# A schedule written out by hand: one pair of the gated block a round later, and the expert groups 4, 2, 2 in place of 2, 4, 2

## The chip, the cores and the metric

The kernel runs on one core of a Trainium2 chip. The metric is the device time of one execution in microseconds, taken as the median of several executions. Engines are named as the profile names them: PE is TensorE (PEld its weight loads), DVE is VectorE, ACT is ScalarE, POOL is GpSimd and SP is SyncE, which here only issues DMAs.

## The reference

The input is 8 sequences of 512 tokens with 128 features. Eight layers follow each other, each added to its input after a layer norm: a recurrence with a circulant matrix, a perceptron with a low-rank addition, a four-layer encoder with linear attention, the same perceptron, and then the four that matter here:

```python
x = x + _L1_attn_a_ref(_layernorm(x), ...)   # causal attention and a perceptron
x = x + _L1_ffn_ref(_layernorm(x), ...)      # experts, first block
x = x + _L1_attn_b_ref(_layernorm(x), ...)   # gated linear attention
x = x + _L1_ffn_ref(_layernorm(x), ...)      # experts, second block
```

In an expert block each token chooses 2 of 8 experts by a router's scores; an expert is `val * silu(gate)` with 352 hidden units and a product back to 128 features, and the two results are added with their softmax weights. The gated block has a short convolution, a gated linear attention in chunks with 64 keys and 256 values, and a normalised product back to 128 features:

```python
h = jnp.einsum('bsd,ehd->bseh', xn, w_up)
val, gate = jnp.split(h, 2, axis=-1)
h = val * jax.nn.silu(gate)
y = jnp.einsum('bseh,edh->bsed', h, w_down)
```

## The kernel before, in words

All eight sequences stay on the chip as one tile `x`; a sequence is four tiles of 128 tokens. The layers up to the first expert block run one after the other and are not touched. What is told here is the last part: the end of the first expert block, the gated block and the second expert block, which are interleaved by hand in `gated_and_experts`.

**An expert block** (`Experts`) splits the sequences into groups (`GROUPS`: the first block 4 and 4, the second 2, 4 and 2 sequences). For each group, in this order:
- `steps(b)` normalises a sequence and makes its router scores (lines 982 to 1035).
- `choose(g)` finds the two experts of each token of the group and the row of each in a list that is sorted by expert. It is a chain of small DVE instructions with two PE products in it (lines 1038 to 1148), in 12 steps.
- `posts(many)` is a stream of indirect DMAs from POOL, one a step. A *slots post* (L1159) writes the rows of one tile of 128 tokens to the sorted list in DRAM, twice for each tile of the group: 16 posts for two sequences, 32 for four. A *given post* (L1171) writes one finished tile's rows back to the order of the tokens. `behind` makes each post wait for the PE instruction that was written last before it.
- `tiles(g)` computes the sorted rows, 128 at a time, with the weights of one expert: 23 tiles for two sequences, 39 for four. It is cut into *pieces*: the first only fetches (`xr`, an SP DMA from the sorted list that waits until every slots post of the group has landed), then one piece for each tile, then two that only finish what is under way. A tile is two products with the up weights (L1274 and L1275), an activation, two DVE products (L1287, L1288), three transposes (L1238), a copy, and the product with the down weights (L1247). Every fourth tile begins with the transposes of a fetched `xr` (L1218).
- `combine(g)` loads the results of each sequence (`y`) and adds them to `x` on DVE (L1324, eight for a sequence); for the second block it also writes the output.

**The gated block** works on pairs of sequences. `gated_steps` gives each pair 25 steps, and the second expert block's `steps` add four. They are named here by their age in the pipeline:
- *norm* (age -1, 2 steps): statistics and normalisation of the two sequences.
- *main* (age 0, 15 steps): transposes (L1630), the up product and a convolution of three DVE instructions each (L1640, L1641, L1647), silu, `vt` (L1678, L1685), the key, query and gate products (L1665), `tau` to `u` on ACT (L1692 to L1696), a series of ten DVE instructions in `u` (L1702, L1704) that ends in `g` (L1720), squares, `pn` (L1725) and `g_nn` (L1731), the logarithm and a scan (L1730 to L1753), `vt` once more with a product (L1760, L1763), and `ke`, `qe` (L1767, L1768).
- *second* (age 1, 8 steps): scores and states (L1776 to L1797), the gate `sg` (L1806, L1807), outputs (L1816 to L1823), the product back and its norm (L1828, L1833, L1837, with a power on POOL through L164 and L165), and the addition to `x` (L1845).
- *end* (age 2, 4 steps): the second expert block's `steps` for the two sequences (L993 to L1031, with a power on POOL, L999).

`pipeline` runs rounds; in each it goes through the list `ages`, 29 places, and at a place with age a it advances the pair that started a rounds ago. Pair 0 has its main step in round 0, pair 1 in round 1, and so on; norms come a round earlier. After each place it also advances a side stream, which `dealt` makes from `tiles`, `posts`, `combine` and `choose`: each has a set of places at which it is advanced, written as `at(round, places)`. `fast(stream, n)` takes n steps at once, `whole` runs a stream to its end. What is left of the side stream after the last round is run alone.

Inside this block `in_program_order` keeps PE, DVE, ACT and POOL each in the order in which the program is written, so that the order above is the order on each engine. Only posts of one kind and group are free among themselves. SP's DMAs are issued in order too.

Afterwards `blend` runs the remaining pieces of the second block's tiles together with given posts and the `combine` of the first two groups; the last group's `combine` is alone at the end.

Of the kernel before, what the change touches and what calls it, by code (L numbers as in the profile page):

```python
# [20 lines left out]
B = 8  # L21
# [1 line left out]
D = 128  # L23
NT = S // P

GROUPS = ((4, 4), (2, 4, 2))
MOST = max(max(g) for g in GROUPS)


# [24 lines left out]
def pipeline(make, count, ages, side=None, every=0, first=0):  # L54

    live = {}
    done = 0
    for now in range(min(ages), count + max(ages)):  # L60
        for age in ages:
            n = now - age
            if 0 <= n < count:
                if n not in live:
                    live[n] = make(n)
                next(live[n], None)
            done += 1
            if side is not None and now >= first and done % every == 0:
                next(side, None)
# [5 lines left out]
@contextmanager  # L75
def in_program_order(tc, *loose):


    block = tc.nc.cur_bb
    first = len(block.bb.instructions)  # L80
    yield
    assert tc.nc.cur_bb is block
    engines = (mybir.EngineType.PE, mybir.EngineType.DVE, mybir.EngineType.Activation, mybir.EngineType.Pool)
    last = {}
    for i in block.bb.instructions[first:]:
        if i.engine in engines:
            group = next((one[i.name] for one in loose if i.name in one), None)
            before = last.setdefault(i.engine, {})
            for other, names in before.items():
                if group is None or other != group:  # L90
                    for name in names:
                        tc.add_manual_dep(i, name, ORDER, reason="the order in which it is written")
            if group is None:
                before.clear()
            before.setdefault(group, []).append(i.name)
# [302 lines left out]
def encoder_block(k):  # L398
# [5 lines left out]
    with tc.tile_pool(name="enc1", bufs=1) as one, tc.tile_pool(name="enc", bufs=2) as pool:  # L404
# [150 lines left out]
        with in_program_order(tc):  # L555
            pipeline(
                steps,
                L * B,
                (2, 0, -1, 3, -2, 1, 0, 2, -1, 4, 1, 0, 2, 1, 0, 2, 1, 0, 3, -2),
            )  # L560
# [340 lines left out]
def blend(*streams):  # L901


    live = [[iter(one), 0, n] for one, n in streams]
    while live:
        one = min(live, key=lambda l: (l[1] + 1) / l[2])
        one[1] += 1
        if next(one[0], live) is live:
            live.remove(one)


def blank_slots(k, groups):

    nc, tc = k.nc, k.tc
    slots = []
    for i, seqs in enumerate(groups):
        n = tiles_of(seqs)
        one = tc.dram_tile([n * P, D + 2], F32, name=f"slots{i}")  # L920
        nc.sync.dma_start(one.rearrange("(t p) d -> p t d", p=P), k.blank[:, None, :].to_broadcast([P, n, D + 2]))
        slots.append((seqs, one, tc.dram_tile([2 * MOST * S + n * P, D], F32, name=f"given{i}")))
    return slots
# [407 lines left out]
def chain(*streams):  # L1331
    for one in streams:
        yield from one


def run(stream):
    for _ in stream:
        pass


def fast(stream, *many):

    while True:
        for n in many:
            for _ in range(n):
                if next(stream, stream) is stream:
                    return
            yield


def idle(many):
    yield from range(many)


def take(stream, many):

    for _ in range(many):
        if next(stream, stream) is stream:
            return
        yield  # L1360


def until(true):

    while not true():
        yield


def whole(stream):

    for _ in stream:
        pass
    yield


def dealt(*streams):

    streams = [(iter(stream), set(steps)) for stream, steps in streams]
    for q in range(1 + max(max(steps) for _, steps in streams)):
        for stream, steps in streams:  # L1380
            if q in steps:
                next(stream, None)
        yield
# [7 lines left out]
def in_turn(m):  # L1391


    streams = [(m.tiles(g), turns(g) - (g.number > 0)) for g in m.groups]

    def pieces():
        for i, (stream, n) in enumerate(streams):
            for at in range(n):
                if at == n - 3 and i + 1 < len(streams):
                    next(streams[i + 1][0])  # L1400
                next(stream)
                yield

    return pieces(), sum(n for _, n in streams)
# [75 lines left out]
def gated_and_experts(k, before, posts, slots, keep, banks, out):  # L1480

    tc = k.tc
    first, last = before.groups
    with tc.tile_pool(name="moe1", bufs=1, side="right") as room:
        m = Experts(k, "n", slots, keep, room, before.p3, out)
        m.hids = before.hids
        one, two, three = m.groups
        tiles, pieces = in_turn(m)
        own = m.posts(sum(2 * g.n + g.tiles for g in m.groups))
        with tc.tile_pool(name="gla1", bufs=1) as alone, tc.tile_pool(name="gla", bufs=2) as pool:  # L1490
            with k.banks(**banks["gated"]):
                gated = gated_steps(k, alone, pool)

                def steps(pair):
                    yield from gated(pair)
                    for _ in zip(m.steps(2 * pair), m.steps(2 * pair + 1)):
                        yield

                ages = (0, 0, 1, 0, 1, 1, 0, 2, 1, 1, 0, 2, 0, 2, 0, -1, 1, 0, 2, 0, 0, 1, -1, 0, 1, 0, 0, 0, 0)

                def at(now, *places):
                    return [(now + 1) * len(ages) + i for i in places]

                side = dealt(  # L1510
                    (before.tiles(last), at(-1, 4, *range(7, 29)) + at(0, *range(0, 29, 2)) + at(1, *range(4))),
                    (posts, at(-1, *range(29)) + at(0, *range(29)) + at(1, *range(6))),
                    (posts, at(-1, *range(9))),
                    (whole(posts), at(1, 6)),
                    (before.combine(first), at(-1, *range(9, 18))),
                    (before.combine(last), at(1, *range(8, 15), 17, 19)),
                    (m.choose(one), at(2, *range(19, 29)) + at(3, *range(3))),
                    (own, at(3, *range(3, 29)) + at(4, *range(29)) + at(5, *range(32))),
                    (own, at(5, *range(0, 32, 2))),
                    (tiles, at(3, *range(20, 29, 2)) + at(4, *range(0, 29, 4)) + at(5, *range(0, 32, 4))),  # L1520
                    (fast(m.choose(two), 2), at(4, *range(19, 26))),
                    (m.choose(three), at(5, *range(19, 32))),
                )
                with in_program_order(tc, before.loose, m.loose):
                    pipeline(steps, B // 2, ages, side=side, every=1)
                    run(side)
        with k.banks(**banks["experts"]), in_program_order(tc, m.loose):
            left = pieces - 21

            def combined(g):  # L1530
                yield from until(lambda: len(g.back) == g.tiles)
                yield from idle(3)
                yield from m.combine(g)

            blend((tiles, left), (take(fast(own, 1, 2), left), left), (chain(*(combined(g) for g in m.groups[:2])), left))
            run(own)
            run(m.combine(three))


def moe_block(k, slots, out=None):  # L1540

    tc = k.tc
    with ExitStack() as stack:
        keep, room = (
            stack.enter_context(tc.tile_pool(name=name, bufs=1, side="right")) for name in ("moe", "moe1")
        )
        m = Experts(k, "m", slots, keep, room, stack.enter_context(tc.tile_pool(name="moe3", bufs=1)), out)
        m.hidden()
        with in_program_order(tc, m.loose):
            for g in m.groups:  # L1550
                pipeline(lambda i: m.steps(g.first + i), g.seqs, (0, -1, 0, 1))
                run(m.choose(g))
                run(m.posts(2 * g.n))
                blend((m.tiles(g), turns(g)), (m.posts(g.tiles), turns(g)))
                run(m.combine(g))
# [538 lines left out]
def net_kernel(ctx: ExitStack, tc: tile.TileContext, drams, offsets, out):  # L2094
# [38 lines left out]
    w_a.close()  # L2133
    slots = [blank_slots(k, one) for one in GROUPS]
    with k.banks(**usual):
# [40 lines left out]
    with tc.If(large > 0):  # L2176
        nc.sync.dma_start(flat, saved)
        slots = [blank_slots(k, one) for one in GROUPS]
        again = ExitStack()
# [228 lines left out]
```

## Time and profile before

| | us |
|---|---|
| median of 7 runs | 2028.75 |
| lowest and highest of them | 2020.35, 2031.98 |
| the profiled execution's own time | 2027.83 |
| its span, first to last instruction | 2026.1 |

| engine | busy us | share of the span |
|---|---|---|
| PE | 1739.6 | 86% |
| PEld | 1180.9 | 58% |
| DVE | 1286.4 | 63% |
| ACT | 948.5 | 47% |
| POOL | 730.8 | 36% |

A busy share is the union of an engine's instructions. Matmuls are pipelined and their ends are modelled, so a busy PE is not PE at its peak. The granted clock is the share of TensorE's full clock that its throttle let through; it was 0.908 over the whole span. A row of a stretch gives its bounds, its length, and each engine's busy time in it (with the number of instructions), then the granted clock, the share of the DMA engines and GB/s. A wait names the instruction that stood, what ended the wait, the sum, the number and the longest. In time lines the columns are start, length, engine, line, operation and tiles; a bracket holds how long the engine had stood before the instruction, and what ended that.

### The profile page before, as it was taken

Reading aid. Unit: us, or ns where it says so; the run is one execution under the profiler, and the core shown is the slowest. Engines: PE = TensorE matmul, PEld = TensorE weight load, DVE = VectorE, ACT = ScalarE, POOL = GpSimd, SP = SyncE. Lnnn points to the kernel's source line nnn. Section 1 sums busy time; section 2 is a strip of 40 time slices with the busy share of each in tenths; the row PEclk is TensorE's granted clock in tenths of the full one; section 3 lists DMA queues with packets and bytes.
Section 4 is the critical chain, followed back from the end, with each engine's and each line's share of the span. In section 5 each row is a group of like instructions: output and inputs, shape, how many; then the busy total and the mean of one; then the engine's idle time right before and its main releaser. Section 6 shows DMA issues by size and latency. Waiting matters only on the chain. (4 is left out here: it accounts for less than half of the span.)

```text
span 2026.1 us, 29976 instructions
## 1 busy us (share of the span) xinstructions
PE 1739.6 (86%) x10171; PEld 1180.9 (58%) x10171; DVE 1286.4 (63%) x4211; ACT 948.5 (47%) x1703; POOL 730.8 (36%) x866
## 2 busy tenths in 40 slices
PE   4998789999998779799999887876989886877995
PEld 2655567788786645344444445654656554655774
DVE  7654788888886664576566635635747775464564
ACT  1022466666664422356556463544554562443553
POOL 2111333333334340244444474561313210447632
PEclk9888799999998878899899898988998886878998
DMA  9900000000000020100000002122100100102332
GB/s 250 162 1 1 1 1 1 1 1 1 1 1 0 1 92 1 42 1 1 1 1 1 9 28 70 57 65 66 39 10 12 48 1 2 50 31 85 100 105 65
DMA packets 79390, 71.25 MB, mean 35 GB/s; under 512 B 6560, under 2 KB 73120, under 8 KB 78336
## 3 DMA queue, kind: packets, MB, share of 16 engines
q1 hardware_dynamic: 69120, 47.89, 9.8%
q0 software_dynamic: 9536, 20.47, 3.0%
q8 instruction: 86, 1.41, 0.3%
q10 hardware_dynamic: 576, 0.90, 0.1%
q14 instruction: 72, 0.59, 0.1%
HBM read 34.98 MB, written 34.25 MB: 34 GB/s over the span
## 5 line engine op out<-in xcount | busy, mean ns | idle before, releaser
L165 POOL TENSOR_TENSOR ln_rs<-rs_v,mhalf 128x4 f32<-128x4 f32 x144 | 150.5, 1046 | 430.6 <-DVE rs_v L164 417.2
L1171 POOL DMA_INDIRECT given<-yr,to x163 | 160.1, 982 | 307.1 <-PE ps_a L1274 110.6
L679 ACT ACTIVATE pr<-ps_s 128x1024 f32<-128x1024 f32 x160 | 154.7, 1019 | 120.9 <-PE ps_s L669 120.8
L1287 DVE SCALAR_TENSOR_TENSOR half<-half,ps_a 128x352 f32<-128x352 f32 x163 | 84.6, 519 | 167.2 <-ACT half L1280 167.0
L1159 POOL DMA_INDIRECT slots<-xn,rpos x128 | 124.4, 972 | 69.8 <-issue 26.0
L1275 PE MATMUL ps_a<-w_m,xt 128*128 x326 | 131.9, 488 | 18.4 <-DVE half L1287 9.9
L669 PE MATMUL ps_s<-qm,rot 32*128 32x128 f32 (+3 forms) x1024 | 124.2, 488 | 23.6 <-ACT pr L679 23.5
L1274 PE MATMUL ps_a<-w_m,xt 128*128 x326 | 135.1, 498 | 7.2 <-ACT xt L1220 5.7
L683 POOL TENSOR_SCALAR_AFFINE_SELECT pr<-pr 128x256 f32<-128x256 f32 x256 | 100.1, 416 | 112.5 <-ACT pr L679 108.3
L530 PEld LDWEIGHTS ps_c<-w_e,mlp_g 128*128 128x128 f32 x1024 | 126.6, 198 | 15.1 <-issue 14.8
L530 PE MATMUL ps_c<-w_e,mlp_g 128*128 128x128 f32 x1024 | 128.8, 281 | 0.1
L1240 ACT COPY gt<-ps_b 128x384 f32<-128x384 f32 x163 | 77.9, 478 | 102.4 <-PE ps_b L1238 102.4
L522 PE MATMUL ps_a<-zt,w_e 128*128 128x512 f32 x256 | 123.7, 607 | 0.9 <-ACT zt L211 0.9
L1280 ACT ACTIVATE half<-ps_a 128x352 f32<-128x352 f32 x163 | 75.5, 463 | 82.7 <-PE ps_a L1274 81.9
L178 DVE BATCH_NORM_AGGREGATE ln_mv<-ln_st 128x2 f32<-128x6 f32 x576 | 100.1, 178 | 16.3
L669 PEld LDWEIGHTS ps_s<-qm,rot 32*128 32x128 f32 x1024 | 59.9, 194 | 82.1 <-ACT pr L679 55.6
L373 ACT ACTIVATE mlp_g<-ps_a,w_col 128x512 f32<-128x512 f32 x64 | 44.0, 687 | 125.5 <-PE ps_a L372 124.8
L523 ACT ACTIVATE mlp_g<-ps_a,w_col 128x512 f32<-128x512 f32 x128 | 85.7, 687 | 35.3 <-PE ps_a L522 35.3
L224 POOL TENSOR_TENSOR xe<-xe,w_erow 128x512 f32<-128x512 f32 x64 | 82.3, 1306 | 55.2 <-DVE ks L480 52.8
L1275 PEld LDWEIGHTS ps_a<-w_m,xt 128*128 128x128 f32 x326 | 62.9, 199 | 63.7 <-DVE half L1287 16.9
L1238 PEld LDWEIGHTS ps_b<-w_ident,hid 128*128 128x128 f32 x489 | 63.5, 145 | 61.9 <-issue 26.9
L211 ACT ACTIVATE zt<-ps_b,w_col 128x512 f32<-128x512 f32 x80 | 62.7, 784 | 75.5 <-PE ps_b L204 75.4
(385 smaller groups left out, 4067.4 us busy)
## 6 DMA issues: line engine op xcount, KB each, us to landing
xr<-slots SPq DMA_DIRECT2D x37, 260.0 KB, 3.0
y<-given SPq DMA_DIRECT2D x32, 256.0 KB, 3.7
slots<-blank SPq DMA_DIRECT2D x3, 2535.0 KB, 29.1
w_m<-in_m_dram SPq DMA_DIRECT2D x2, 2244.0 KB, 10.6
w_e<-in_e_dram SPq DMA_DIRECT2D x2, 1700.0 KB, 11.0
slots<-blank SPq DMA_DIRECT2D x2, 1495.0 KB, 30.6
given<-yr,to POOLq DMA_INDIRECT x163, 2.2
x<-in_u_dram SPq DMA_DIRECT2D x8, 256.0 KB, 9.5
```

Of the source, the lines that this page charges most:

```text
L165: nc.gpsimd.tensor_tensor(out, v, self.mhalf[:, :n], ALU.pow)
L178: nc.vector.bn_aggr(mv[:, t, :], st[:, t, :])
L522: nc.tensor.matmul(ph, w1[:, c * P : (c + 1) * P], ht, start=True, stop=True)
L523: nc.scalar.activation(g[:, c, :], ph, AF.Relu, bias=col["e_b1"][:, l, c : c + 1])
L530: nc.tensor.matmul(py[:, t, :], g[:, c, t * P : (t + 1) * P], w2[:, c, :], start=(c == 0), stop=(c == 3))
L669: nc.tensor.matmul(halves[g // 2][:, g % 2, at : at + S - u * P], kr[rows, u * P : (u + 1) * P], qm[rows, i, u * P : S], start=True, stop= ...
L679: nc.scalar.activation(pr, sc, AF.Exp)
L683: nc.gpsimd.affine_select(out=v, in_=v, pattern=[[0, 2], [1, P]], compare_op=ALU.is_ge, fill=0.0, base=0, channel_multiplier=-1,)
L1159: made = nc.gpsimd.indirect_dma_start(out=g.slots, out_offset=bass.IndirectOffsetOnAxis(ap=g.pos[:, i, t : t + 1], axis=0), in_=g.xn[:, t, :],
L1171: made = nc.gpsimd.indirect_dma_start(out=g.given, out_offset=bass.IndirectOffsetOnAxis(ap=to, axis=0), in_=yr, in_offset=None,)
L1274: nc.tensor.matmul(pg, xt, w["experts"][:, bass.ds(o + HID, HID)], start=True, stop=True)
L1275: nc.tensor.matmul(pv, xt, w["experts"][:, bass.ds(o, HID)], start=True, stop=True)
```

## The change

`pipeline` takes a list of the rounds in which the pairs start in place of their number. The gated block's pairs now start in rounds 0, 1, 3 and 4. The first block's second group of tiles, until now dealt over two rounds and four places, is spread over three, and its posts and `combine` come later. The second block's groups are 4, 2 and 2 sequences in place of 2, 4 and 2; `choose` of the first group is taken two steps at a time, its 32 slots posts follow, and the tiles stand at every second place of the last round and of what is run after it, until 31 pieces (21 before) are done. Sizes, instructions and transfers of a tile, a pair or a post stay as they are.

```diff
-GROUPS = ((4, 4), (2, 4, 2))
+GROUPS = ((4, 4), (4, 2, 2))
...
-    for now in range(min(ages), count + max(ages)):
+    starts = {start: n for n, start in enumerate(range(count) if isinstance(count, int) else count)}
+    for now in range(min(ages), 1 + max(starts) + max(ages)):
         for age in ages:
-            n = now - age
-            if 0 <= n < count:
+            n = starts.get(now - age)
+            if n is not None:
...
                 side = dealt(
-                    (before.tiles(last), at(-1, 4, *range(7, 29)) + at(0, *range(0, 29, 2)) + at(1, *range(4))),
-                    (posts, at(-1, *range(29)) + at(0, *range(29)) + at(1, *range(6))),
+                    (before.tiles(last), at(-1, 4, *range(7, 23)) + at(0, *range(0, 29, 2)) + at(1, *range(0, 28, 3))),
+                    (posts, at(-1, *range(29)) + at(0, *range(29)) + at(1, *range(29))),
                     (posts, at(-1, *range(9))),
-                    (whole(posts), at(1, 6)),
+                    (whole(posts), at(2, 1)),
                     (before.combine(first), at(-1, *range(9, 18))),
-                    (before.combine(last), at(1, *range(8, 15), 17, 19)),
-                    (m.choose(one), at(2, *range(19, 29)) + at(3, *range(3))),
-                    (own, at(3, *range(3, 29)) + at(4, *range(29)) + at(5, *range(32))),
-                    (own, at(5, *range(0, 32, 2))),
-                    (tiles, at(3, *range(20, 29, 2)) + at(4, *range(0, 29, 4)) + at(5, *range(0, 32, 4))),
-                    (fast(m.choose(two), 2), at(4, *range(19, 26))),
-                    (m.choose(three), at(5, *range(19, 32))),
+                    (before.combine(last), at(2, *range(3, 12))),
+                    (fast(m.choose(one), 2), at(3, *range(19, 26))),
+                    (own, at(3, *range(26, 29)) + at(4, *range(29)) + at(5, *range(29)) + at(6, *range(32))),
+                    (tiles, at(5, 0, *range(2, 29, 2)) + at(6, *range(0, 32, 2))),
+                    (fast(m.choose(two), 2), at(5, *range(19, 26))),
+                    (fast(m.choose(three), 2), at(6, *range(19, 26))),
                 )
...
-                    pipeline(steps, B // 2, ages, side=side, every=1)
+                    pipeline(steps, (0, 1, 3, 4), ages, side=side, every=1)
...
-            left = pieces - 21
+            left = pieces - 31
```

## The prediction, made before the run

> **What bounds the kernel now.** I read the page's slices first, then a table of stretches that I cut at the last product of each main step (DVE's `qe`, L1768), then the waits and the time lines of PE, POOL and DVE at the joints between stretches.
>
> From the page, PE's busy tenths and the granted clock in 40 slices:
>
> ```profile
> PE   4998789999998779799999887876989886877995
> ...
> PEclk9888799999998878899899898988998886878998
> ```
>
> PE is the engine to follow; in the last third (slices 27 to 38, everything that the change touches) it falls to 6 and 7 in two places. The table of stretches says where:
>
> ```profile
> core 0: us, PE busy (x) PEld busy (x) DVE busy (x) ACT busy (x) POOL busy (x), PEclk, DMA share, GB/s
> 1360.30:1462.80 102.50, 82.16 (x389) 54.64 (x390) 64.32 (x173) 52.83 (x107) 25.88 (x25) 0.90 0.21 58
> 1462.80:1563.90 101.10, 89.97 (x477) 61.37 (x475) 57.18 (x140) 49.29 (x96) 22.64 (x21) 0.92 0.04 13
> 1563.90:1639.90 76.00, 66.91 (x339) 44.54 (x337) 58.20 (x163) 42.12 (x75) 15.66 (x13) 0.87 0.11 34
> 1639.90:1715.50 75.60, 56.77 (x275) 37.62 (x275) 47.44 (x139) 31.73 (x52) 7.23 (x5) 0.80 0.00 1
> 1715.50:1756.50 41.00, 32.30 (x187) 25.18 (x187) 15.83 (x59) 14.18 (x27) 21.77 (x20) 0.75 0.16 46
> 1756.50:1835.20 78.70, 65.49 (x323) 49.45 (x324) 51.68 (x194) 35.27 (x84) 35.29 (x36) 0.83 0.13 37
> 1835.20:1852.80 17.60, 5.50 (x34) 4.13 (x33) 1.89 (x7) 3.20 (x9) 13.36 (x14) 0.69 0.33 99
> 1852.80:2004.10 151.30, 145.10 (x850) 111.08 (x851) 85.85 (x232) 82.76 (x198) 78.89 (x82) 0.99 0.31 90
> ```
>
> Rows 1 to 5 are rounds 0 to 4 of the gated block (1360.3 to the second block's first expert tile at 1756.5: 396.2 us by the rows' bounds), rows 6 to 8 that block's 85 tiles. With tiles beside it a round is near PE's limit (82 of 102, 90 of 101); round 3 has no tile and PE works 57 of 76, DVE 47: no engine is full, the pair's chain of steps is the limit. In row 7 PE stands still:
>
> ```profile
> 1838.04 1.72 PE L1247 MATMUL ps_y<-w_m,gt 128*128 x12
> 1850.94 1.09 PE L1218 MATMUL ps_b<-w_ident,xr 128*128 128x128 f32 x4 [11.18 <-DMA xr<-slots]
> ```
>
> (time line: start, length, instruction, idle before.) Group two's first tiles wait for its 32 posts.
>
> **First, where things land.** `pipeline` advances the side stream only from round 0 on (`first=0`), so a place that is written `at(n, ...)` runs in round n+1. The trace shows it: pair 0's transposes (round 0, place 0) are at 1360.4, the first tile of `before.tiles(last)` at 1376.2. Pieces are calls of a tile stream; the first only fetches, the last two only drain. By real rounds, old to new:
> - round 0: 23 pieces to 17; round 1: 15 and 15, pair 2's norm leaves; round 2: 4 to 10, pair 2's main step leaves, combine(last) leaves.
> - round 3: old pairs 1 (end), 2 (second step), 3 (main), choose(one). New: pair 1 end, pair 2 main, combine(last), no tile.
> - round 4: new pair 2 second, pair 3 main, choose(one), no tile. Round 5: pair 2 end, pair 3 second, 29 posts, no tile. Round 6: pair 3 end and 14 tiles; 16 more are dealt after the pipeline.
>
> No arithmetic goes or comes (23+39+23 tiles become 39+23+23). Only overlap changes.
>
> **Round by round.** Work of one pair, summed over its lines' groups in those stretches: main step PE 25 to 34, DVE 26, ACT 19 to 24; second step PE 22 to 27, DVE 10; end PE 4.7, DVE 5.6, ACT 6. choose: DVE 9.1 for 8 tiles, 11.5 for 16.
> - Round 0: six tiles stood between pn and `qe`, where g_nn (1443.2) to `qe` (1462.8) took 19.6; in round 2, without tiles, the same took 12.0 (1627.8 to 1639.9). So -7 (bounds -4 and -13, six tiles of 2.2): 95.5.
> - Round 1: DVE's 4.7 of norm goes, partly under PE: -2 (0 to -5): 99.
> - Round 2: old round 4 is the same two steps without tiles: 36.6 from 1715.5 to the end of PE's last L1837 at 1752.1, PE 32 of it. Added: eight tiles of 2.2, 2 of draining, less some 7 of PE's gaps and low clock (0.75): 49 (bounds 42, PE's bare sum at full clock, and 56, nothing filled).
> - Round 3: pair 2's main step without another pair's second step. Its chain from rows: convolution on DVE to 12.5, then combine's adds 10.7 and the end step's 6.5 on DVE to about 30; ACT's end step to 32.6 and tau to u 4.3: the series starts at 37 (old: 42.6 in round 2). Series, pair 3's norm and g to 48; logarithm and products to 54; vt 3.2 and ke, qe 1.3: 59 (bounds 54 and 68). The y loads land while DVE convolves (post 1.3, landing 2.3, load 4), as in old round 2, where none of DVE's waits names them; uncovered they would cost up to 7.
> - Round 4: old round 3 (75.6) less the end step of a pair on PE (L1024 1.1, L1030 3.6) and its delay of sg (1.3), plus choose at 16 tiles and whole: 11.5 against 7.4: 75.6-6+4.1 = 74. Below: DVE's sum 26+10+11.5 and the 8.9 it waits for the exponential, 56; above: 80, if choose's matmul wait repeats per step.
> - Round 5 to the first tile: PE as in old round 4, 36.6. What follows is posts. Old joint:
>
> ```profile
> 1748.00 0.95 POOL L1159 DMA_INDIRECT slots<-xn,rpos  x1 [0.30 <-issue]
> 1749.26 0.96 POOL L1159 DMA_INDIRECT slots<-xn,rpos  x1 [0.30 <-issue]
> 1750.21 1.84 PE L1837 MATMUL ps_b<-ones_col,sg 128*128 128x1 f32 x16
> 1754.69 1.09 PE L1218 MATMUL ps_b<-w_ident,xr 128*128 128x128 f32 x4 [2.63 <-DMA xr<-slots]
> 1756.55 1.54 PE L1274 MATMUL ps_a<-w_m,xt 128*128 x2 [0.78 <-ACT xt L1220]
> ```
>
> Old: 16 posts, all issued before PE's last L1837 ended. New: 32, the last eight at places 21 to 28, and each post waits for the PE instruction written before it (`behind`), which from place 21 on is that L1837. So after 36.6: the pow (1.0, POOL's queue), eight posts of 1.26 (0.96 and 0.30 of issue) 10.1, landing 2.3, xr 3.0, then L1218 and its copy 1.9, with the small steps between: 19 against 4.4 now. Behind those posts on POOL nothing waits but given posts; on PE, DVE and ACT the tiles stand first in order, so pair 3's end cannot fill the hole. 36.6+19 = 55.6 (bounds 52 and 60).
>
> Sum: 95.5+99+49+59+74+55.6 = 432.1 against 396.2: first tile **+36** us.
>
> **The 85 tiles.** Undisturbed, tiles follow each other every 2.27 (L1274 at 1898.10 and 1941.2, 19 apart). From 1756.5 to the last one's 2001.5: 245 = 84 x 2.27 + 54. The 54: 28.4 up to 1830.4 (pair 3's end, choose two and three), 15.3 in row 7, 10.5 later (3.5 of it at the second joint, 1943.4 to 1949.2). New: group two needs 16 posts, and they go out while 16 tiles run, so its joint costs 3.5: -12. Pair 3's end gets one tile more over its latency and choose(two) is 2.4 narrower: -4 (bounds 0 and -15). Sum **-16**. The last group is two sequences as before, so the 22 after the last tile stay.
>
> Net +36-16 = +20. The profiled execution took 2027.83 (span 2026.1), 0.9 under the median 2028.75: 2027.8+20 = **2048**.
>
> **A rule against the change.** The granted clock is 0.99 in row 8, and 0.80 and 0.75 in rounds 3 and 4; L1274's pair takes 0.76 in a steady run and 1.54 after row 7's hole. The new rounds 3 to 5 have fewer matmuls per us than any old round but the fourth. At old round 4's clock against old round 2's, round 3's chain through PE (some 14 us of it) would take 2 more, inside its bounds. [...]
>
> **The rivals.**
> - *Longer still* (0.18): rounds 3 to 5 take their upper bounds, because PE is cold and steps of two pairs block each other in order: 9+6+4 more: 2067. For it: DVE waits 9.2 us for L1837 in old round 3. Against: fewer steps meet there now.
> - *Not slower* (0.20): DVE, not the crossing of PE's queue, limits a two-pair round once the third pair is gone; round 4 falls from 74 to its 56: -18, 2030, no change; with the tiles' other bound (11 more) 2019. It decides below 60 us for round 4. For it: round 3 is PE-ordered in these waits; against: the chain alone is 59, and choose's matmuls stand in it.
> - *Not what it says*: "beside the last rounds" holds for one gated round only, by the shift above; that is in the sum.
>
> ```profile
> DVE rs_v L164 <- PE ps_b L1837: 9.2, 2, 6.1
> DVE pol L1704 <- ACT u L1696: 8.9, 1, 8.9
> ```
>
> (DVE's waits in old round 3: total, times, longest.)
>
> **How the numbers follow.** Slower by about 20: 0.62, alone 2037 to 2060. With the rivals: low 2024 leaves out half of "not slower", high 2064 half of "longer still". About 0.3%, 6 us, is what a measurement of this kernel can tell from no change: "not slower" divides into 0.10 faster and 0.10 same, and 0.02 of the main case ends in same: slower 0.78.
>
> **What would show it.** Right: the first block's last L1274 near 1600 (1568.8 before) and the second block's first one near 1792; about 19 us between the last L1837 and it, with eight POOL posts in a row 1.26 apart; no wait of L1218 over 3 us at the first joint of groups; round 3 near 59, round 4 near 74. Wrong: a first tile before 1775, or a round 4 under 60; or tiles that run at 2.27 through choose two and three, which would take back 20 us.

## The result, and the profile after

The changed kernel takes 2043.71 us (median of 18 runs, 2035.5 to 2048.1) against 2028.84 (46 runs): ratio 1.0075, 95% interval 1.0064 to 1.0085, so 13 to 17 us slower. 2048 was forecast, with 2024 to 2064 as its range. The profiled execution took 2047.26 with a span of 2045.5.

The part ahead of the gated block is the same in all these kernels, but its length differs from profile to profile: in those taken on chips where the kernel before takes 2027 us, pair 0's transposes start between 1353.6 and 1361.4. So I count stretches from those transposes on: before 665.8 us (1360.3 to 2026.1), changed 687.1 (1358.4 to 2045.5), +21.3; in a second profile of the changed kernel 681.7, +15.9, and that is the size of the medians' difference.

The table of stretches of the changed kernel, cut at the same instructions (`qe` is now at L1770): rounds 0 and 1, round 2 up to pair 2's transposes, rounds 3, 4 and 5 up to the first tile of the second block, then 30 tiles, the other 55, and what follows the last tile's start:

```profile
core 0: us, PE busy (x) PEld busy (x) DVE busy (x) ACT busy (x) POOL busy (x), PEclk, DMA share, GB/s
1358.40:1452.90 94.50, 75.29 (x332) 49.22 (x333) 59.07 (x159) 48.22 (x94) 20.61 (x20) 0.84 0.20 57
1452.90:1551.60 98.70, 86.99 (x454) 59.61 (x453) 51.82 (x113) 45.52 (x86) 17.47 (x17) 0.91 0.05 15
1551.60:1605.10 53.50, 47.89 (x307) 37.17 (x306) 29.28 (x100) 25.41 (x57) 17.31 (x16) 0.94 0.03 12
1605.10:1664.20 59.10, 41.58 (x140) 23.04 (x138) 45.62 (x137) 31.76 (x54) 9.23 (x8) 0.74 0.13 40
1664.20:1738.10 73.90, 54.29 (x251) 35.80 (x251) 46.54 (x114) 26.26 (x39) 9.07 (x8) 0.78 0.02 5
1738.10:1794.10 56.00, 33.38 (x187) 25.64 (x187) 16.42 (x60) 14.02 (x26) 31.80 (x31) 0.68 0.15 47
1794.10:1868.50 74.40, 67.43 (x362) 51.14 (x362) 43.51 (x159) 39.66 (x94) 33.09 (x33) 0.91 0.19 52
1868.50:2020.90 152.40, 141.80 (x828) 108.21 (x829) 89.62 (x263) 79.56 (x192) 77.92 (x81) 0.99 0.30 87
2020.90:2045.50 24.60, 4.59 (x31) 3.49 (x30) 6.76 (x21) 2.58 (x8) 4.79 (x5) 0.69 0.29 84
```

| stretch | before | forecast | changed | changed, second profile |
|---|---|---|---|---|
| round 0 | 102.5 | 95.5 | 94.5 | 93.5 |
| round 1 | 101.1 | 99 | 98.7 | 97.4 |
| round 2 | 76.0 | 49 | 53.5 | 53.6 |
| round 3 | 75.6 | 59 | 59.1 | 59.0 |
| round 4 | (to first tile) 41.0 | 74 | 73.9 | 71.4 |
| round 5 to the first tile | - | 55.6 | 56.0 | 55.2 |
| sum to the first tile | 396.2 | 432.1 | 435.7 | 430.1 |
| first to last tile | 245 | 229 | 226.8 | 226.9 |
| after the last tile's start | 24.6 | 24.6 | 24.6 | 24.7 |

Rounds 3, 4 and 5 have no tile, and the granted clock is 0.68 to 0.78 there; they last 189 us. The kernel before had no tile in rounds 3 and 4 (116.6 us up to its first one, at 0.80 and 0.75), and none in most of round 2. From the first block's last tile to the second block's first it was 187.7 us before (1568.8 to 1756.5) and is 194.5 now (1599.6 to 1794.1): the stretch without tiles is hardly longer, it begins later. The hole at the end of round 5, on PE and on POOL:

```profile
1773.79 1.98 PE L1839 MATMUL ps_b<-ones_col,sg 128*128 128x1 f32 x16
1792.26 1.09 PE L1219 MATMUL ps_b<-w_ident,xr 128*128 128x128 f32 x4 [16.50 <-DMA xr<-slots]
1794.13 1.54 PE L1275 MATMUL ps_a<-w_m,xt 128*128 x2 [0.78 <-ACT xt L1221]
```

```profile
1775.50 0.96 POOL L1160 DMA_INDIRECT slots<-xn,rpos  x1 [0.30 <-issue]
1776.47 1.05 POOL L166 TENSOR_TENSOR g_rs<-rs_v,mhalf 128x4 f32<-128x4 f32 x1
1777.71 1.04 POOL L1160 DMA_INDIRECT slots<-xn,rpos  x1 [0.19 <-issue]
1779.05 0.96 POOL L1160 DMA_INDIRECT slots<-xn,rpos  x1 [0.30 <-issue]
...
1786.63 0.96 POOL L1160 DMA_INDIRECT slots<-xn,rpos  x1 [0.30 <-issue]
```

After the power, eight posts go out, 1.26 apart, the last at 1786.6; 18.3 us pass from the end of L1839 to the first tile. The joint of groups one and two, where the kernel before stood for 11.18 on a fetch, now has the fetch in time and waits for a copy alone:

```profile
1908.52 1.72 PE L1248 MATMUL ps_y<-w_m,gt 128*128 x12
1910.08 0.60 PE L1219 MATMUL ps_b<-w_ident,xr 128*128 128x128 f32 x4
1911.46 0.86 PE L1275 MATMUL ps_a<-w_m,xt 128*128 x2 [0.78 <-ACT xt L1221]
```

### The profile page after: what moved, and what is told of

Its sections match the earlier page's. It is cut to its first block, busy times and chain, and to the rows that moved or that the text cites. A ratio compares the mean times of both kernels' runs of the same rounds, so it can differ in the third digit from the quotient of the medians.

```text
span 2045.5 us, 29961 instructions
## 1 busy us (share of the span) xinstructions
PE 1743.2 (85%) x10171; PEld 1180.2 (58%) x10171; DVE 1287.1 (63%) x4211; ACT 948.5 (46%) x1703; POOL 727.0 (36%) x866
## 4 chain that ended last, share of the span: by engine, by line
PE 32%; DVE 13%; ACT 6%; issue 2%; DMA 1%; POOL 1%; DVEq 0%; POOLq 0%; SPq 0%; ACTq 0%
PE ps_a L1275 4%; PE ps_a L1276 4%; PE ps_s L670 3%; PE ps_y L1248 3%; PE ps_b L1239 2%; PE ps_o L699 2%; PE ps_a L1248 2%; DVE sh L1649 1%; ACT pr L680 1%; DVE x L1325 1%; PE ps_c L891 1%; PE ps_a L1667 1%; PE ps_a L1818 1%; DVE half L1288 1%; PE ps_b L1839 1%
## 5 line engine op out<-in xcount | busy, mean ns | idle before, releaser
L1275 PE MATMUL ps_a<-w_m,xt 128*128 x326 | 136.3, 502 | 11.5 <-ACT xt L1221 7.0
L531 PEld LDWEIGHTS ps_c<-w_e,mlp_g 128*128 128x128 f32 x1024 | 126.6, 198 | 15.1 <-issue 14.8
L670 PEld LDWEIGHTS ps_s<-qm,rot 32*128 32x128 f32 x1024 | 59.1, 192 | 82.4 <-ACT pr L680 56.3
L225 POOL TENSOR_TENSOR xe<-xe,w_erow 128x512 f32<-128x512 f32 x64 | 82.2, 1305 | 55.2 <-DVE ks L481 52.8
```

The lines of the kernel that those rows point to most:

```text
L531: nc.tensor.matmul(py[:, t, :], g[:, c, t * P : (t + 1) * P], w2[:, c, :], start=(c == 0), stop=(c == 3))
L670: nc.tensor.matmul(halves[g // 2][:, g % 2, at : at + S - u * P], kr[rows, u * P : (u + 1) * P], qm[rows, i, u * P : S], start=True, stop= ...
L1275: nc.tensor.matmul(pg, xt, w["experts"][:, bass.ds(o + HID, HID)], start=True, stop=True)
```

## The experiments

The runs were taken on chips of two kinds: on two chips the kernel before took 2026.8 and 2027.3 us, on two others 2065.9 and 2065.1. Times from different chips are compared as ratios to the kernel before on the same chip, and even these shift (see "Places as the rounds they name").

### Posts a round earlier

```diff
-(fast(m.choose(one), 2), at(3, *range(19, 26))),
-(own, at(3, *range(26, 29)) + at(4, *range(29)) + ...),
+(fast(m.choose(one), 2), at(2, *range(19, 26))),
+(own, at(2, *range(26, 29)) + at(3, *range(29)) + at(4, *range(29)) + ...),
```

> Changed kernel, but choose(one) and its 32 slots posts one round earlier (round 3 and 4 by the trace's rounds), all else the same. Theory (the loss is in part the hole of 18.3 us between the last L1839 at 1775.8 and the first tile at 1794.1, made by posts that are issued too late): the posts go out during round 4's 74 us, the fetch is long done, the hole shrinks to 2 to 4 us. Choose's 11.5 us of DVE move from round 4 (74 to 69) to round 3 (59 to 66). Sum -13: 2031 us (2026 to 2036). Rival (the hole is only where the waiting shows; pair 3's end and a cold PE take its place): the tiles start at most 4 us earlier or run slower afterwards, 2040 us or more.

2028.71, ratio 1.0000 (0.9985 to 1.0015): the whole loss is back. The two runs below that keep the late posts took 2041.2 and 2042.5 on the same chip. Its stretches of rounds 3, 4 and 5, and PE at the end of round 5:

```profile
1605.80:1675.40 69.60, 43.70 (x142) 24.83 (x140) 56.73 (x182) 31.43 (x54) 13.70 (x12) 0.71 0.12 37
1675.40:1738.90 63.50, 51.43 (x248) 32.37 (x247) 35.68 (x70) 26.75 (x39) 32.87 (x31) 0.85 0.09 30
1738.90:1777.90 39.00, 32.91 (x187) 25.31 (x187) 14.72 (x51) 14.03 (x26) 5.24 (x4) 0.76 0.08 21
```

```profile
1774.65 2.00 PE L1839 MATMUL ps_b<-ones_col,sg 128*128 128x1 f32 x16
1776.52 0.63 PE L1219 MATMUL ps_b<-w_ident,xr 128*128 128x128 f32 x4
```

L1219 follows L1839 without a stop. Choose's work changed rounds (DVE 45.6 to 56.7 and 46.5 to 35.7), and rounds 3 and 4 together took 133.1 instead of 133.0. So the hole is 17 us by itself, and nothing took its place: the tiles took 227.6 after it, 226.8 in the changed kernel.

### Two posts a place

```diff
+(own, at(4, *range(8, 19))),
```

> Changed kernel with two posts at each of places 8 to 18 of round 5, so that all 32 are written before the last L1839. Theory A (behind: the eight posts of places 21 to 28 wait for the last PE instruction): the hole shrinks by eight posts of 1.26, -10: 2034 us. Theory B (POOL's own rate: 11 posts are done by place 7, the other 21 take 26.5 us and two powers 2, whatever they wait for): the last post ends at some 46 instead of 49.5 us of the round, -3: 2041 us (2037 to 2046), with the powers of pair 3 later in the queue.

2041.24, ratio 1.0075 (1.0054 to 1.0096). In its profile the hole is 14.8 (L1840 ends at 1771.0, first tile at 1785.8), 3.5 shorter:

```profile
1765.68 3.58 PE L1836 MATMUL ps_c<-down_n,sh 128*128 128x128 f32 x16
1769.06 1.96 PE L1840 MATMUL ps_b<-ones_col,sg 128*128 128x1 f32 x16
1783.93 1.09 PE L1219 MATMUL ps_b<-w_ident,xr 128*128 128x128 f32 x4 [12.91 <-DMA xr<-slots]
```

```profile
1769.91 0.95 POOL L1160 DMA_INDIRECT slots<-xn,rpos  x1 [0.30 <-DMA slots<-xn,rpos]
1771.17 0.96 POOL L1160 DMA_INDIRECT slots<-xn,rpos  x1 [0.30 <-issue]
1772.14 1.04 POOL L166 TENSOR_TENSOR g_rs<-rs_v,mhalf 128x4 f32<-128x4 f32 x1
1773.39 1.03 POOL L1160 DMA_INDIRECT slots<-xn,rpos  x1 [0.20 <-issue]
```

POOL is back to back from 1750.5 on: theory B. The eight posts stood behind L1839, but without that wait POOL's 32 x 1.26 would have ended only 3.5 earlier. A prediction from `behind` alone would have got this edit wrong by 7 us.

### The first block's tiles not spread

```diff
-at(-1, 4, *range(7, 23)) + at(0, *range(0, 29, 2)) + at(1, *range(0, 28, 3))
+at(-1, 4, *range(7, 29)) + at(0, *range(0, 29, 2)) + at(1, *range(4))
```

> Changed kernel with the first block's tiles where they were: 23, 15 and 4 pieces in rounds 0, 1 and 2 instead of 17, 15 and 10. Theory (round 2 pays more for six tiles, 53.5 against 36.6 without any, than round 0 saves, 7 to 8): round 0 near 102, round 2 near 42, -4: 2040 us (2036 to 2045). Rival (the spread fills PE's gaps in round 2, and is what keeps the change from costing more): +5, 2049 us.

2042.49, ratio 1.0069 (1.0051 to 1.0087): no difference from the change. The time lies in the theory's range, and rounds 0 and 2 came near what it said, but neither its gain of 4 nor the rival's loss of 5 is there. Rounds 0, 1 and 2, together 247.3 us against 246.7:

```profile
1354.80:1458.40 103.60, 84.47 (x389) 55.84 (x390) 64.41 (x173) 52.79 (x107) 25.89 (x25) 0.87 0.20 58
1458.40:1561.50 103.10, 90.61 (x478) 63.18 (x477) 53.03 (x115) 48.25 (x92) 19.46 (x19) 0.90 0.04 13
1561.50:1602.10 40.60, 35.10 (x225) 28.05 (x223) 20.34 (x74) 16.96 (x36) 12.42 (x12) 0.87 0.12 36
```

Six tiles in round 2 cost 53.5 - 40.6 = 12.9, that is 2.15 each, nearly their full 2.27; taken from rounds 0 and 1 they save 9.1 and 4.4. The spread moves work and changes nothing.

### The groups without the delay

```diff
-pipeline(steps, (0, 1, 3, 4), ages, side=side, every=1)
+pipeline(steps, B // 2, ages, side=side, every=1)
```

with the first block's side stream as before and each place of the second block one round earlier.

> Kernel before with the groups 4, 2, 2 and the second block's choose, posts and tiles placed as in the changed kernel, but one round earlier, with the pairs in consecutive rounds and the first block's tiles as before: the change without the delay of pairs 2 and 3. Theory (delay and spread cost some 20, groups and places cancel: the hole +14, whole choose +4, the joint and the tiles -18): 2029 us (2022 to 2036). Rival (late posts and groups are the loss, the delay is free): 2040 us or more.

2022.09, ratio 0.9974 (0.9962 to 0.9986), at the lower edge of the theory's range. Rounds 0 to 4:

```profile
1354.30:1456.70 102.40, 81.89 (x389) 54.50 (x390) 64.33 (x173) 52.76 (x107) 25.85 (x25) 0.90 0.20 58
1456.70:1557.80 101.10, 89.97 (x477) 61.65 (x476) 57.22 (x140) 49.27 (x96) 22.64 (x21) 0.92 0.04 13
1557.80:1636.10 78.30, 68.69 (x339) 46.02 (x337) 58.24 (x164) 41.99 (x75) 15.65 (x13) 0.84 0.11 33
1636.10:1710.40 74.30, 55.50 (x275) 36.37 (x275) 52.06 (x146) 32.15 (x54) 12.86 (x10) 0.80 0.02 5
1710.40:1769.70 59.30, 37.02 (x187) 29.14 (x187) 16.45 (x60) 14.02 (x26) 31.80 (x31) 0.64 0.14 44
```

From the transposes to the end it takes 666.9, the kernel before 665.8, the changed one 687.1. So the delay of pairs 2 and 3 with the spread costs 20.2: round 2's 78.3 becomes 53.5 + 59.1 = 112.6, rounds 0 and 1 give 10.3 back, rounds 4 and 5 (133.6 here as rounds 3 and 4) give 3.7. Groups and places cancel in the trace: the hole is paid here too (59.3 against 41.0), the tiles take 227.0 instead of 245.

The same kernel once more, since its median is lower than before's and its trace is not:

> The groups, posts and tiles of the change without the delay of pairs 2 and 3, once more. Its first trace counts 666.9 us from pair 0's transposes to the end, the kernel before 665.8, but its median was 0.26% under before. Theory (no difference: what was gained lies in the part ahead, which differs from execution to execution): 0.998 to 1.002. Rival (a real gain): 0.996 to 0.9985.

Ratio 0.9926 (0.9904 to 0.9948), on a chip where the kernel before took 2065: below both expectations, on the rival's side. Both chips show a gain, but its trace puts it neither in the rounds (102.0, 101.7, 78.1 and 74.3 for the first four) nor, on the first chip, anywhere after the transposes. In the first chip's two profiles it lies ahead of the transposes (1354.3 against 1360.3), where nothing was changed and where profiles differ by 8 us anyway. What makes it stays open; a profile of the kernel before on the second chip would be needed.

### Places as the rounds they name

```diff
-ages, side=side, every=1)
+ages, side=side, every=1, first=-1)
```

> Changed kernel with the side stream advanced from round -1 on, so that a place written for round n runs in round n: every tile, post, choose and combine one round earlier against the pairs. Theory (the loss lies in where the tiles and posts stand against the pairs, not in the delay as such: the second block's tiles then run beside pair 3's second and end steps, the posts go out in the 74 us of pair 3's main step, no hole): -12 to -20, 2027 us (2018 to 2036). Rival (a round more of gated steps costs its 20 whatever stands beside it): 2040 us or more.

Ratio 0.9953 (0.9935 to 0.9971), on the slower chip. On the other:

> The changed kernel with places run in the rounds that they name, once more, beside the run above and the changed kernel on one chip: 0.995 of before again if that ratio doesn't hang on the chip; theory for its profile: no hole before the second block's first tile.

> The changed kernel as it is, on the same chip: 1.0075 of before again; stretches as in its first profile within 3 us each.

2033.07 (1.0026, 1.0008 to 1.0044) beside 2039.08 for the changed kernel (1.0065, 1.0047 to 1.0083). The ratio of one kernel hangs on the chip by 0.7%, so no order between runs on different chips finer than that is claimed. On one chip the aligned places win back 6 of the 12 us that the change costs there, half of the least that was expected. The hole is gone, as was expected:

```profile
1748.69 0.63 PE L1781 MATMUL ps_b<-w_ident,ke 128*128 128x128 f32 x2
1749.92 1.09 PE L1219 MATMUL ps_b<-w_ident,xr 128*128 128x128 f32 x4 [0.60 <-DMA xr<-slots]
1751.79 1.54 PE L1275 MATMUL ps_a<-w_m,xt 128*128 x2 [0.78 <-ACT xt L1221]
```

The expectation for the changed kernel's second profile held (within 3 us in each stretch, 2.5 in round 4).

### The kernel before, its places aligned or its choose earlier

> Kernel before with the same: the side stream from round -1 on. Theory: its tile-less round 3 gets posts and five tiles, round 4 eight; but the 23 tiles of round -1 run with no pair beside them, and combine(last) comes right after its last tiles in round 1, with a wait there. Gain 10 to 25 at the end, loss some 10 at the start: 2020 us (2010 to 2032). Rival: the order in the before kernel was no loss, 2029 or more.

> Kernel before with one line changed: choose(two) one round earlier (round 4), so that group two's 32 posts begin before group one's tiles. Theory (the 15.3 us stop of the tiles at the joint of groups one and two was posts issued too late, which is what the groups 4, 2, 2 cured): the joint costs 3.5, -12, and choose's DVE work (11.5) leaves the tiles' stretch for round 4: 2015 us (2010 to 2022). Rival (posts are POOL-bound and push group one's given posts and the powers back; the stop only moves): within 4 us of before.

> The run with choose(one) a round earlier (2028.7 us), and in it ten pieces of the second block's tiles moved into round 5, beside pair 2's end and pair 3's second step, where PE worked 33 of 56 us. Theory (tile-less rounds leave PE idle, tiles fill it): round 5 grows by some 13, the tiles after it need 22 less: -9, 2020 us (2014 to 2026). Rival (tiles in the round lengthen the chain by as much as they take): 2027 us or more.

All three ran on one slower chip: 0.9972 (0.9952 to 0.9992), 0.9963 (0.9944 to 0.9983) and 0.9971 (0.9952 to 0.9989), where the aligned change has 0.9953 (the groups alone have 0.9926 on another slower chip). As ratios these lie in the ranges of their theories, but the two kernels that ran on both kinds of chip had ratios lower by 0.5 and 0.7% on the slower kind, which is as much as these effects; so only the profiles count here.

The kernel before with its places aligned took 81.8, 73.6, 77.1 and 87.7 in rounds 0 to 3, and some 65 in the round ahead of them, where its tiles run without a pair. Round 3, with five pieces of tiles, is 12 longer than the 75.6 that it took without (on the other kind of chip). With choose(two) earlier the first joint shrank from 17.6 between tiles to 8.4, and its first fetch came in time, so late posts had made that stop; a wait of 3.34 for a copy is left:

```profile
1869.85 0.60 PE L1218 MATMUL ps_b<-w_ident,xr 128*128 128x128 f32 x4
1873.79 1.54 PE L1274 MATMUL ps_a<-w_m,xt 128*128 x2 [3.34 <-ACT xt L1220]
```

In the run with tiles in round 5 that round took 54.4 to the last L1839, instead of 37.8 on the other kind of chip: the seven tiles that start in it cost 16.6, or 2.4 each. What they save later is not shown, since no run without them was profiled on that chip.

### The second block a round earlier, pairs as before

```diff
-(m.choose(one), at(2, *range(19, 29)) + at(3, *range(3))),
+(m.choose(one), at(1, *range(19, 29)) + at(2, *range(3))),
 ...
-(tiles, at(3, *range(20, 29, 2)) + at(4, *range(0, 29, 4)) + at(5, *range(0, 32, 4))),
+(tiles, at(2, *range(20, 29, 2)) + at(3, *range(0, 29, 4)) + at(4, *range(0, 29, 4)) + at(5, *range(0, 32, 4))),
 ...
```

> Kernel before with the whole second block one round earlier (choose(one) straight after pair 0's end step, its posts in round 3, eight more pieces of tiles, five in round 3 and eight each in rounds 4 and 5; choose(two) in round 4, choose(three) in round 5); pairs in consecutive rounds, groups 2, 4, 2, first block as before. Theory (what costs is PE standing in rounds 3 and 4 and at the joints while posts are late; no delay of pairs is needed to fill them): rounds 3 and 4 take tiles into their 28 us of idle PE, the joint's 15.3 goes: 0.990 to 0.995 of before. Rival (tiles lengthen the pair's chain as much as they fill): 0.998 or more.

2033.17, ratio 1.0027 (1.0011 to 1.0043): the rival. Rounds 2 and 3:

```profile
1563.50:1647.00 83.50, 67.13 (x339) 46.05 (x338) 64.69 (x201) 39.61 (x71) 15.53 (x13) 0.84 0.10 31
1647.00:1734.60 87.60, 74.97 (x321) 48.77 (x322) 47.15 (x125) 38.90 (x67) 23.20 (x21) 0.75 0.10 28
```

Choose in round 2 adds 7.5 to it, and tiles between the steps of round 3 add 12: PE waits for what stands ahead of it in order (in round 3 5.2 for `yr` before L1760, which round 3 of before does not have; after it 8.1 for `gt` before L1024), and one fetch after round 3 is still 7.3 late. Idle PE in a round of dependent steps was not free room here.

## Why the prediction was right

- **Where things land.** The shift of a round stood in the trace of before, and the change's profile follows it: the first block's last L1275 at 1599.6 (1600 said), the second block's first at 1794.1 (1792 said).
- **Rounds 0 and 1**: -8.0 and -2.4 against -7 and -2. **Round 3**: 59.1 for 59, **round 4**: 73.9 (71.4 in the second profile) for 74, **round 5 with its hole**: 56.0 for 55.6; the hole 18.3 for 19, with eight posts 1.26 apart. Sums made along the chain, from rows of another round, held to a few us.
- **The hole's reason** was only half right. The prediction let the eight posts wait for the last L1837 (`behind`). But POOL was still busy with earlier posts when that product (now L1839) ended at 1775.8, and with them and the power it came free only at 1777.5; and the run with two posts a place shows that `behind` was worth 3.5 us, not the 10 of eight posts. That the two limits ended within 2 us of each other is why the number came out: luck.
- **Round 2** is the term that was mis-sized: 49 said, 53.5 measured. The step that failed is "less some 7 of PE's gaps and low clock": eight tiles and the draining added 16.9 to the 36.6, of the 19.6 that they would take with nothing filled, so 2.7 was saved. PE stood for 5.6 us of round 2, as it had for 5.4 of the same steps without tiles, and the run without the spread shows 2.15 of 2.27 paid for each of six of these tiles. It was inside its bound of 56.
- **The tiles**: 226.8, a surplus of 36.1 over 84 x 2.27, for 38; the joint's 11.18 went, as said.
- **The net** was +20; medians say +15, the two profiles +21.3 and +15.9. The sum is right for an execution like the first profile, some 5 us too much for the median.
- **The clock.** The mean granted clock was 0.74, 0.78 and 0.68 in rounds 3 to 5, against 0.80 and 0.75 in rounds 3 and 4 before. PE ran slowly on round 3's chain: over the two products below the granted clock was 0.55; with tiles about, the same products take 1.93 (round 2) and 3.65 (round 1) at 1.00. But in round 2 of the kernel before they had 0.55 as well. First before, then changed:

```profile
1611.08 3.72 PE L1030 MATMUL ps_b<-w_m,xnt 128*128 128x8 f32 x16
1614.73 6.33 PE L1665 MATMUL ps_a<-sh,w_g 128*64 128x512 f32 x16
```

```profile
1638.95 3.58 PE L1031 MATMUL ps_b<-w_m,xnt 128*128 128x8 f32 x16 [5.96 <-ACT xnt L1027]
1642.46 6.27 PE L1667 MATMUL ps_a<-sh,w_g 128*64 128x512 f32 x16
```

The rows from which the sum was made held the low clock already; the argument against the change set the means of two whole rounds (0.75 in round 4 before, 0.87 in round 2) against each other for the products on the chain, so its 2 us would have priced the low clock a second time.

- **Round 3's path** was not quite the one in the sum. DVE's series began 33.2 us into the round, not at 37, and ended at 44.5, not 48; but then DVE waited for these products and for the logarithm behind them, and went on at 49.5. The early series and the waits cancelled, so the exact 59 is luck in part:

```profile
DVE g_nn L1733 <- PE ps_b L1727: 1.7, 1, 1.7
DVE pol L1739 <- ACT lg L1732: 1.5, 1, 1.5
```

- **"Not slower"** needed round 4 under 60: it was 73.9, and still 63.5 with choose taken out of it. **"Longer still"** needed rounds 3 to 5 at their upper bounds; none came near.

What the prediction did not see: the hole was not part of the idea. With the same choose a round earlier, which pair 1's end allows, the change cost nothing (1.0000); and without the delay of pairs 2 and 3 the groups 4, 2, 2 were faster than the kernel before (0.9974 and 0.9926 on two chips), for a reason that the traces do not show. So either step takes the loss away: dropping the delay, which cost 20.2 with the posts late, or keeping it and posting a round earlier, which gave 17 back.

## What to carry to other kernels

Before costing a schedule, find in the trace of before in which round its places really run; here every label was one round off, and with the delay in place a stream of posts began a round later than it could, which was worth 17 us. A delay by a round is paid where a round loses its partner: 78 us for two pairs' steps together became 113 for the two apart. Posts that a fetch waits for are costed twice, once by what each is queued behind and once by the issuing engine's rate (1.26 us a post here), and the later of the two counts. A low clock is priced by the clock of the products on the chain (0.55 in round 3 here), in the rows that the sum uses, not by the mean of the round (0.74).

## What was not expected of the hardware

The kernel before took 2027 us on two chips and 2065 to 2066 on two others, and the ratio of one kernel differs by 0.5 to 0.7% between the kinds. The two profiles of the groups without the delay, one of each kind, agree in rounds 0 to 3 within 0.6 us each, but round 4 to the first tile took 59.3 on the faster and 55.7 on the slower chip, the second block's tiles 227.0 and 239.9, and pair 0's transposes came at 1354.3 and 1372.6; what makes the difference stays open. On the faster kind, round 2 repeated as 53.5, 53.5, 53.4 and 53.6 us in the four profiles of three kernels that have it unchanged, while the unchanged part ahead moved by 8.
